# A decoder layer with soft-routed experts on one core: constants loaded from SyncE's queue, self scores in two parts and steps taken by sequence, ahead of the first expert

## The chip, the cores and the metric

The kernel runs on one core of one Trainium2 chip. The metric is device time in microseconds. Before the change the median of 7 runs is 2962.05 us (2960.71 to 2966.57). The engines are named as in the profile: PE (TensorE's matmuls), PEld (its weight loads), DVE (VectorE), ACT (ScalarE), POOL (GpSimd) and SP (SyncE). SP and ACT each have a queue from which they start DMA transfers.

## The reference

One decoder layer in float32 on x of 32 sequences x 100 tokens x 256, with a context of 361 tokens per sequence:

```python
x = x + self_attention(layernorm(x))          # 16 heads of 16, rope on q and k, causal
x = x + cross_attention(layernorm(x), ctx)    # 16 heads of 16, with biases, 361 keys
x = x + soft_moe(layernorm(x))                # 8 experts x 128 slots, hidden size 1024

def soft_moe(x):
    xn, sn = rmsnorm(x) * gamma, rmsnorm(slot_embeds) * slot_gamma
    logits = einsum("bnd,esd->bnes", xn, sn)
    dispatch = softmax(logits, axis=tokens)
    combine = softmax(logits, axis=(experts, slots))
    slots = einsum("bnd,bnes->besd", xn, dispatch)
    eo = gelu(slots @ w1 + b1) @ w2 + b2      # one w1 and w2 for each expert
    return einsum("bmd,bnm->bnd", eo, combine)
```

## The kernel before, in words

The 32 sequences form 8 groups of 4. For each group the kernel runs the 8 experts one after the other (`run_expert`, L1456): the first layer `ph` in 8 chunks of 512 columns, gelu on ACT into `hT`, the second layer `pe`, and `py`, which combines the result into x. A group needs its preparation first: self attention and cross attention of its 4 sequences, the logits `lt` (`prepare`, L1281) and the routing (`route`, L1376). The preparation of group g+1 is laid between the matmuls of group g's experts. Group 0 has no expert to lie behind: all of its preparation stands ahead of the first `ph`. This stretch is what the change is about. While it is recorded, `state["group"]` is -1.

**How the order is made.** The kernel is written as generators ("streams"): `self_attention`, `cross_softmax`, `crossing`, `cross_queries`, `cross_context`, and `prepare`. Each yields a `Need` (L299): the buffers that its next step reads and the PSUM banks that it takes. While the program is recorded, a planner keeps an estimated time for PE (`pe["t"]`) and a list of jobs for DVE, ACT, POOL and SP, each with an estimated duration, and writes the instructions out in the order of these estimates. `drive` (L344) takes the first stream in its list whose needs are met by the planner's time. `idle_from` (L82) says from when on the planner takes each engine to be free, and the numbers given to `load_raw` and `written` say when it takes a load to have landed. None of this costs time on the chip: it decides the order on each engine, and each engine then works through its order strictly, waiting on semaphores.

**The head.** `load_x(0)` is put on SP's list. `load_constants` (L459) starts 17 transfers from ACT's queue: four self attention weights (`rawWk`, `rawWq`, `rawWv`, `rawWo`), the rope table, five parts of `rows` (biases and gammas), four cross attention weights (`xwWk` and so on), two bias rows for all partitions, and the slot embeddings `se`. SP starts x of group 0 and 1 and the contexts. The DMA starts use eight completion semaphores in turn: the built program lets the start of a transfer wait until the transfer with the same semaphore, the eighth before it over both queues, has landed. PE transposes the raw weights (`turn_raw`, L445), the first context (`ps_cT`) and the first normalized sequence (`ps_xhT`), and ACT copies the last two out of PSUM.

**Self attention of a sequence** (`self_attention`, L862): `turned` (layer statistics on DVE and POOL, `xh` on POOL, `ps_xhT` on PE, its copy on ACT), `rotation` (`ps_qk`, then rope on DVE and POOL and `rotk` on ACT), `self_v` (`ps_v`), `self_scores` (L747), `self_turn` (`ps_pT`), `self_values` (`ps_av`) and `project_out` (`ps_o`). `self_scores` takes both PSUM pairs (`sc0`, `sc1`, two banks each, 8 heads each) and issues its 8 matmuls (fp32, so two passes each) over the four 32-row strips of PE, q = 0 to 3 for each of two chunks; then for each half: mask (`p`) and maximum on DVE, subtraction on POOL, exp on ACT, sum on DVE.

**Cross attention of a sequence**: `cross_context` makes keys and values (`ps_cT`, `ps_kT`, `ps_xv`), `cross_queries` the queries (`ps_xq`, `xqT`), and `cross_softmax` the scores in four "quads"; for a quad each of two halves takes a PSUM pair, has a maximum on DVE (`xnmax`) and two exps on ACT. For the first four sequences PE transposes the result (`ps_xpT`, 12 transposes a quad, copied by DVE, ACT, DVE); for all later ones DVE transposes it in PSUM into `xt` (one buffer), and two DMAs through DRAM (`xd`, `xpT`) lay it out. `crossing` multiplies by the values (`ps_xav`), projects (`ps_o`) and starts the tokens' statistics, which end with `xn` on POOL.

**The tail.** After the fourth crossing: `xn`, `ps_xhT`, `xnT`, `ps_lt` with maxima `mx`, transposes of the logits into both PSUM pairs, `cnm`, `diag`, `ps_nm`, then `route` for expert 0: exps, the sum `sm` and its reciprocal on DVE, `dT` on POOL, `pd`, `disp`, `sl`, `slT`, and then `ph`. L1588 drives this routing alone.

`near` (L857) limits how far ahead of the current group a stream may go: with the group at -1, one sequence into group 1, whatever the caller asks for.

## Time and profile before

| | |
|---|---|
| median of 7 runs | 2962.05 us |
| the profiled execution | 2963.34 us |
| its span, first to last instruction | 2961.6 us |
| granted TensorE clock, mean | 0.995 |
| PE busy, share of the span | 2911.1 us, 98% |
| PEld busy | 2035.9 us, 69% |
| DVE busy | 1367.9 us, 46% |
| ACT busy | 1234.9 us, 42% |
| POOL busy | 555.9 us, 19% |
| `ph` and `pe` matmuls, busy | 964.2 us and 1000.8 us |
| first `ph` starts | 220.83 us |

A line of a view by time gives start and duration in us, engine, source line, operation, the tiles written and read, their shapes, the count of instructions merged, and in brackets the idle time of that engine before them and what ended it. "ACTq" and "SPq" are the engines' sequencers starting a DMA. In a view by stages each engine has its busy time and its count of instructions; a granted clock of 0.5 means that TensorE ran at half its full rate. Busy times of PE are those of pipelined matmuls whose ends are modelled. Helpers record most instructions, so that nearly all matmuls carry line L268 and all transposes L272; the tile names tell them apart.

### The profile page before, as it was taken

Reading aid. Unit: us, or ns where it says so; the run is one execution under the profiler, and the core shown is the slowest. Engines: PE = TensorE matmul, PEld = TensorE weight load, DVE = VectorE, ACT = ScalarE, POOL = GpSimd, SP = SyncE. Lnnn points to the kernel's source line nnn. Section 1 sums busy time; section 2 is a strip of 40 time slices with the busy share of each in tenths; the row PEclk is TensorE's granted clock in tenths of the full one; section 3 lists DMA queues with packets and bytes.
Section 4 is the critical chain, followed back from the end, with each engine's and each line's share of the span. In section 5 each row is a group of like instructions: output and inputs, shape, how many; then the busy total and the mean of one; then the engine's idle time right before and its main releaser. Section 6 shows DMA issues by size and latency. Waiting matters only on the chain.

```text
span 2961.6 us, 42941 instructions
## 1 busy us (share of the span) xinstructions
PE 2911.1 (98%) x17393; PEld 2035.9 (69%) x17393; DVE 1367.9 (46%) x2719; ACT 1234.9 (42%) x2662; POOL 555.9 (19%) x722
## 2 busy tenths in 40 slices
PE   6989999999999999999999999999999999999999
PEld 5756766767667676677667666677676766677676
DVE  5764554546443554436444355444554345422121
ACT  3554444444443444434444444433444434433331
POOL 3413231032101221013210222002321021000000
PEclk9989999999999999999999999999999999999999
DMA  3012433334351343414343243433344234422221
GB/s 111 12 70 69 166 103 121 133 117 169 109 179 68 130 148 125 157 58 151 133 156 119 98 150 126 147 111 119 123 156 141 92 105 162 167 72 71 72 75 52
DMA packets 191574, 343.58 MB, mean 116 GB/s; under 512 B 8104, under 2 KB 160656, under 8 KB 191376
## 3 DMA queue, kind: packets, MB, share of 16 engines
q1 hardware_dynamic: 187632, 337.18, 33.3%
q10 hardware_dynamic: 3744, 3.65, 0.4%
q8 instruction: 138, 2.26, 0.3%
q14 instruction: 60, 0.49, 0.0%
HBM read 249.44 MB, written 91.36 MB: 115 GB/s over the span
## 4 chain that ended last, share of the span: by engine, by line
PE 95%; ACT 2%; DVE 1%; DMA 1%; POOL 1%; issue 0%; SPq 0%; ACTq 0%; DVEq 0%; POOLq 0%
PE pe L268 31%; PE ph L268 30%; PE sc L268 4%; PE sl L268 4%; PE py L268 4%; PE ps_lt L268 3%; PE ps_xv L268 3%; PE ps_kT L268 3%; PE ps_xav L268 2%; PE ps_qk L268 2%; PE ps_o L268 2%; PE ps_pT L272 1%; PE pd L272 1%; PE sc L272 1%; PE ps_xq L268 1%; PE ps_v L268 1%
## 5 line engine op out<-in xcount | busy, mean ns | idle before, releaser
L268 PE MATMUL pe<-w,hT 128*128 128x256 f32 x4096 | 1000.8, 383 | 0.0
L268 PE MATMUL ph<-slT,w 128*128 128x512 f32 x2048 | 964.2, 599 | 1.6 <-ACT hT L1479 1.4
L268 PEld LDWEIGHTS pe<-w,hT 128*128 128x128 f32 x4096 | 742.1, 190 | 156.4 <-issue 52.7
L1479 ACT ACTIVATE hT<-ph,cols 128x512 f32<-128x512 f32 x512 | 350.7, 687 | 799.1 <-PE ph L268 798.9
L268 PEld LDWEIGHTS ph<-slT,w 128*128 128x128 f32 x2048 | 372.0, 190 | 325.2 <-issue 291.2
L1049 ACT ACTIVATE sc<-sc,xnmax 128x361 f32<-128x361 f32 x448 | 237.8, 531 | 146.0 <-DVE xnmax L1039 138.8
L1039 DVE TENSOR_REDUCE xnmax<-sc 128x2 f32<-128x722 f32 x256 | 222.2, 904 | 162.7 <-PE sc L268 162.1
L1063 DVE STREAM_TRANSPOSE xt<-sc 128x384 f32<-128x384 f32 x448 | 231.8, 556 | 23.6 <-ACT sc L1049 18.2
L608 POOL TENSOR_SCALAR ve<-bnmv 100x1 f32<-100x1 f32 x96 | 27.8, 290 | 904.8 <-DVE bnmv L605 904.6
L1417 POOL TENSOR_TENSOR dT<-dT,ri 128x400 f32<-128x400 f32 x64 | 54.6, 853 | 721.4 <-DVE ri L1414 720.3
L1531 DVE SCALAR_TENSOR_TENSOR x<-py,cinv,x 100x256 f32<-100x256 f32 x256 | 112.7, 477 | 153.0 <-PE py L268 152.1
L1409 DVE TENSOR_REDUCE sm<-dT 128x4 f32<-128x400 f32 x64 | 34.7, 543 | 264.5 <-ACT dT L1400 264.5
L787 POOL TENSOR_TENSOR p<-p,nmax 100x800 f32<-100x800 f32 x64 | 96.5, 1524 | 315.4 <-DVE nmax L780 312.4
L1508 DVE TENSOR_TENSOR eo<-pe,b 128x512 f32<-128x512 f32 x128 | 87.6, 685 | 129.1 <-PE pe L268 128.8
L268 PEld LDWEIGHTS sl<-disp,xn 100*128 100x128 f32 x1024 | 135.7, 194 | 8.1 <-issue 1.3
L268 PE MATMUL sl<-disp,xn 100*128 100x128 f32 x1024 | 136.7, 277 | 0.9 <-DVE disp L1430 0.9
L1446 DVE TENSOR_SCALAR slT<-sl,cols 128x512 f32<-128x512 f32 x128 | 95.4, 745 | 84.3 <-PE sl L268 83.5
L268 PE MATMUL py<-eo,cT 128*100 128x256 f32 x512 | 131.5, 379 | 0.8 <-DVE eo L1508 0.8
L268 PE MATMUL sc<-kT,xqT 32*128 32x361 f32 x1024 | 124.6, 514 | 3.3 <-DVE xt L1063 2.0
L770 DVE TENSOR_TENSOR p<-sc,causal 100x800 f32<-100x800 f32 x64 | 60.4, 985 | 137.8 <-PE sc L268 137.8
L428 ACT ACT_TABLE_LOAD x93 | 119.3, 1283 | 1.6
L268 PEld LDWEIGHTS py<-eo,cT 128*100 128x100 f32 x512 | 85.4, 167 | 50.0 <-issue 29.0
(144 smaller groups left out, 3237.8 us busy)
## 6 DMA issues: line engine op xcount, KB each, us to landing
w<-in_L_ffn_w_dram SPq DMA_DIRECT2D x128, 1024.0 KB
xd<-xt SPq DMA_DIRECT2D x112, 768.0 KB
xpT<-xd SPq DMA_DIRECT2D x112, 768.0 KB
ctx<-in_ctx_dram SPq DMA_DIRECT2D x32, 256.0 KB
b<-in_L_ffn_b_dram SPq DMA_DIRECT2D x64, 128.0 KB
ctx<-in_ctx_dram SPq DMA_DIRECT2D x32, 105.0 KB
x<-in_x_dram SPq DMA_DIRECT2D x8, 400.0 KB
out_dram<-x SPq DMA_DIRECT2D x16, 200.0 KB
```

The lines of the kernel that those rows point to most:

```text
L268: nc.tensor.matmul(out, lhsT=lhsT, rhs=rhs, **kw)
L272: nc.tensor.transpose(out, in_, identity)
L428: act(0.2, lambda: nc.scalar.activation(spare, mhalf[:1, :1], f), [], [], table=table, prio=2)
L770: lambda i=i, hs=hs: nc.vector.tensor_tensor(p.get()[:, hs, :].rearrange("n (q h) k -> n q h k", q=2), sc[i].get()[:S, :, : HG * S].rearra ...
L787: lambda hs=hs: nc.gpsimd.tensor_tensor(p.get()[:, hs, :], p.get()[:, hs, :], nmax.get()[:, hs].unsqueeze(2).to_broadcast([S, HPC, S]), AL ...
L1039: lambda nm=nm, sc=sc: nc.vector.tensor_reduce(nm.get(), sc.get()[:, :, :SK], axis=AX.X, op=ALU.max, negate=True),
L1049: nc.scalar.activation(to[:, :SK], sc.get()[:, i, :SK], AF.Exp, bias=nm.get()[:, i : i + 1], accum_out=sums.get()[:, c, q, r : r + 1],)
L1063: nc.vector.transpose(t_.get()[:, :, :, 2 * t + i, :].rearrange("p j c u -> p c j u"), sc.get()[:, i, : NKB * P].rearrange("p (c u j) -> p ...
L1446: lambda dc=dc, sl=sl: nc.vector.tensor_scalar(slT.get()[:, dc, : nb * NS], sl.get()[:, : nb * NS], cols.ap[:, NGM + dc : NGM + dc + 1], N ...
L1479: lambda h=h, ph_=ph_, hc=hc: nc.scalar.activation(h.get()[:, :n], ph_.get()[:, :n], AF.Gelu, bias=cols.ap[:, e * NHC + hc : e * NHC + hc ...
L1508: lambda eo=eo, po=po, m=m: nc.vector.tensor_tensor(eo.get()[:, :m], po.get().rearrange("p (i d) -> p i d", i=2)[:, :m], b2.unsqueeze(1).t ...
L1531: lambda b=b, i=i: nc.vector.scalar_tensor_tensor(xs[g].get()[:, b, :], py[:S, i, :], k.ci.get()[:, b : b + 1], xs[g].get()[:, b, :], ALU. ...
```

## The change

- `load_constants`: ACT's queue starts `rawWk`, `rawWq` and the rope table only. The other 14 transfers go to SP's queue, in another order: `rawWv`, `xwWk`, the five parts of `rows`, `rawWo`, `xwWv`, the two bias rows, `xwWq`, `xwWo`. The slot embeddings become a job of SP (`load_slots`), and stand in the built program behind x of group 1 and the second context. x of group 0 and the first context are started ahead of the constants.
- `self_scores` becomes a generator. For group -1 it takes one PSUM pair at a time and issues the four matmuls of each half by themselves; for later groups both halves are issued as before.
- `drive` takes, among the streams that could go on, the one whose next step belongs to the lowest sequence (steps that belong to none count as 0), not the first in the list. It serves the stretch ahead of the first expert and the ends of later experts; the filling between an expert's matmuls keeps the list's order.
- `near` allows the caller's distance in group -1 too: self attention may begin up to three sequences into group 1.
- The routing ahead of the first expert is driven together with the other streams.
- `idle_from` and the landing times that the planner assumes are changed.

In the built program 1003 matrix instructions stand ahead of the first `ph`, where 987 did: those of the sixth sequence's `ps_xhT`, `ps_qk`, `ps_v` and half of its scores are added. The total is unchanged. Three quads of the fifth sequence stand between `ps_lt` and `pd`, where they stood ahead of `ps_lt`.

```diff
@@ -79,7 +79,7 @@
     COL, PIPE, HOP, LOAD = 0.00084, 0.25, 0.15, 1.28
     pe = {"t": 0.0, "slow": 1.25}
     waiting = {e: [] for e in ("DVE", "ACT", "POOL", "SP")}
-    idle_from = {"DVE": 0.0, "ACT": 8.0, "POOL": 6.0, "SP": 0.0}
+    idle_from = {"DVE": 0.0, "ACT": 3.0, "POOL": 5.0, "SP": 0.0}
     tables = {"now": None, "gelus": 0}
 
     class Buf:
@@ -283,6 +283,7 @@
             p, tag = self.pools[(len(self.past) - 1) % len(self.pools)]
             return p.tile([P, 512], F32, tag=tag, name=name)
 
+    at = {}
     rings = {
         "small": Banks([(ps_m, "mm"), (ps_b, "big")]), "big": None,
         "pairs": Kept(
@@ -302,7 +303,7 @@
 
         def __init__(self, *reads, banks=1, pairs=0, exps=None, when=None, t=0.0):
             self.reads, self.banks, self.pairs = reads, banks, pairs
-            self.exps, self.when, self.t = exps, when, t
+            self.exps, self.when, self.t, self.seq = exps, when, t, 0
 
         def time(self):
             items = [w for b in self.reads for w in b.writes]
@@ -319,8 +320,8 @@
     class Steps:
 
 
-        def __init__(self, it):
-            self.it, self.need, self.result = it, Need(banks=0), None
+        def __init__(self, it, seq=None):
+            self.it, self.need, self.result, self.seq = it, Need(banks=0), None, seq
 
         def blocked(self):
             return self.it is None or (self.need.when is not None and not self.need.when())
@@ -336,6 +337,7 @@
             reads = self.need.reads
             try:
                 self.need = next(self.it)
+                self.need.seq = at.get(self.seq, 0)
             except StopIteration as end:
                 self.it, self.result = None, end.value
             for b in reads:
@@ -348,7 +350,7 @@
             run()
             ready = [s for s in streams if s.fits()]
             if ready:
-                ready[0].step()
+                min(ready, key=lambda s: s.need.seq).step()
             else:
                 advance(*(s.time() for s in streams))
         return goal.result
@@ -435,12 +437,17 @@
         return t.rearrange("k (m r d) -> k m r d", r=2, d=DK)
 
 
-    def load_raw(nm, at):
+    def load_raw(queue, nm, at):
         raw = R["hT"].new(f"raw{nm}")
         v = raw.get().rearrange("p (c d) -> p c d", c=ND)
-        nc.scalar.dma_start(out=v, in_=a[f"L0_attn_{nm}"].rearrange("(c p) d -> p c d", p=P))
+        queue.dma_start(out=v, in_=a[f"L0_attn_{nm}"].rearrange("(c p) d -> p c d", p=P))
         raw.written(at)
         raws[nm] = raw
+
+    def load_cross(nm, at):
+        w = wT["x" + nm] = fixed([P, ND, D], f"xw{nm}")
+        nc.sync.dma_start(out=w.ap, in_=a[f"L0_xattn_{nm}"].rearrange("(c p) o -> p c o", p=P))
+        w.written(at)
 
     def turn_raw(nm):
 
@@ -458,11 +465,11 @@
 
     def load_constants():
 
-        load_raw("Wk", 5.5)
-        load_raw("Wq", 8.0)
+        load_raw(nc.scalar, "Wk", 5.0)
+        load_raw(nc.scalar, "Wq", 6.5)
         nc.scalar.dma_start(out=rope, in_=a["rope"].rearrange("p (m f) n -> p m f n", f=2))
-        load_raw("Wv", 11.0)
-        load_raw("Wo", 12.5)
+        load_raw(nc.sync, "Wv", 9.0)
+        load_cross("Wk", 10.0)
         rows = Buf(ap=one.tile([P, P], F32, name="rows"))
         for r0, src in (
             (BQ, a["L0_xattn_bq"].rearrange("(c p) -> c p", p=P)),
@@ -471,20 +478,25 @@
             (NGM, a["L0_ffn_norm_gamma"].rearrange("(c p) -> c p", p=P)),
             (SGM, a["L0_ffn_slot_norm_gamma"].rearrange("(c p) -> c p", p=P)),
         ):
-            nc.scalar.dma_start(out=rows.ap[r0 : r0 + src.shape[0], :], in_=src)
-        rows.written(14.0)
-        for k, nm in enumerate(("Wk", "Wq", "Wv", "Wo")):
-            w = wT["x" + nm] = fixed([P, ND, D], f"xw{nm}")
-            nc.scalar.dma_start(
-                out=w.ap, in_=a[f"L0_xattn_{nm}"].rearrange("(c p) o -> p c o", p=P)
-            )
-            w.written(15.5 + 1.5 * k)
-        nc.scalar.dma_start(out=bvB, in_=a["L0_xattn_bv"].partition_broadcast(P))
-        nc.scalar.dma_start(out=boB, in_=a["L0_xattn_bo"].partition_broadcast(P))
+            nc.sync.dma_start(out=rows.ap[r0 : r0 + src.shape[0], :], in_=src)
+        rows.written(13.0)
+        load_raw(nc.sync, "Wo", 14.0)
+        load_cross("Wv", 15.0)
+        nc.sync.dma_start(out=bvB, in_=a["L0_xattn_bv"].partition_broadcast(P))
+        nc.sync.dma_start(out=boB, in_=a["L0_xattn_bo"].partition_broadcast(P))
+        load_cross("Wq", 17.5)
+        load_cross("Wo", 18.5)
         se = Buf(ap=wpool.tile([P, NE, D], F32, tag="w1", name="se"))
-        nc.scalar.dma_start(out=se.ap, in_=a["L0_ffn_slot_embeds"].rearrange("e s d -> s e d"))
-        se.written(26.0)
         return rows, se
+
+    def load_slots(se):
+        job(
+            "SP", 0.4,
+            lambda: nc.sync.dma_start(
+                out=se.ap, in_=a["L0_ffn_slot_embeds"].rearrange("e s d -> s e d")
+            ),
+            [], [se], lag=8.0,
+        ).deps.append(18.0)
 
     def make_constants():
 
@@ -750,18 +762,28 @@
         p = R["p"].new()
         sums, nmax, rinv = R["sums"].new(), R["nmax"].new(), R["rinv"].new()
         qT = t.get().rearrange("p (m c n) -> p m c n", m=2, c=ND)[:, 0]
-        sc = [rings["pairs"].new("sc") for _ in range(2)]
-        for c in range(ND):
-            for q in range(NQ):
-                rows_ = slice(q * 32, (q + 1) * 32)
-                matmul(
-                    sc[q // 2].get()[:S, q % 2, c * 2 * S : (c + 1) * 2 * S],
-                    lhsT=qT[rows_, c, :],
-                    rhs=kT.get()[rows_, c, :, :],
-                    share=NQ, start=True, stop=True,
-                )
-        parts = []
+        sc, parts = {}, []
+        pairs_ = ((0,), (1,)) if state["group"] < 0 else ((0, 1),)
+
+        def issue(ts):
+            for i in ts:
+                sc[i] = rings["pairs"].new("sc")
+            for c in range(ND):
+                for i in ts:
+                    for q in (2 * i, 2 * i + 1):
+                        rows_ = slice(q * 32, (q + 1) * 32)
+                        matmul(
+                            sc[i].get()[:S, q % 2, c * 2 * S : (c + 1) * 2 * S],
+                            lhsT=qT[rows_, c, :],
+                            rhs=kT.get()[rows_, c, :, :],
+                            share=2 * len(ts), start=True, stop=True,
+                        )
+
         for i in range(2):
+            for ts in pairs_:
+                if ts[0] == i:
+                    yield Need(t, kT, banks=0, pairs=len(ts), exps=(4.0, 8.0))
+                    issue(ts)
             hs = slice(i * HPC, (i + 1) * HPC)
             part, s1, m1 = p.part(), sums.part(), nmax.part()
             parts.append(part)
@@ -857,7 +879,7 @@
     def near(b, ahead):
 
         last = FIRST[state["group"] + 1] + SIZES[state["group"] + 1]
-        return b < last + (ahead if state["group"] >= 0 else 1)
+        return b < last + ahead
 
     def self_attention(rows):
 
@@ -883,11 +905,11 @@
 
         yield from begin(0)
         for b in range(B):
+            at["self_attention"] = b
             xhT, t, kT = begun.pop(b)
             yield Need(xhT, wT["Wv"])
             self_v(xhT)
-            yield Need(t, kT, banks=0, pairs=2, exps=(4.0, 8.0))
-            p, parts, wide = self_scores(t, kT)
+            p, parts, wide = yield from self_scores(t, kT)
             if b == 0:
                 yield Need(raws["Wo"])
                 turn_raw("Wo")
@@ -1139,6 +1161,7 @@
     def cross_queries():
 
         for b in range(B):
+            at["cross_queries"] = b
             yield free(lambda: near(b, 1) and b in selfed and b < 2 + len(queried))
 
             def bias(b=b):
@@ -1155,6 +1178,7 @@
     def cross_context():
 
         for b in range(B):
+            at["cross_context"] = b
             yield free(lambda: near(b, 1))
             cT, keys[b] = yield from context(b)
             yield free(lambda: state["valued"] >= b - 1)
@@ -1164,6 +1188,7 @@
     def cross_softmax():
 
         for b in range(B):
+            at["cross_softmax"] = b
             for i, (c, r) in enumerate(QUADS):
                 n = b * len(QUADS) + i
                 yield free(
@@ -1270,6 +1295,7 @@
     def crossing():
 
         for b in range(B):
+            at["crossing"] = b
             g, i = WHERE[b]
             yield free(lambda: g <= state["group"] + 1)
             if i == 0:
@@ -1560,13 +1586,17 @@
 
     state = {"group": -1, "valued": -1, "crossed": -1, "turned": 0, "flipped": 0, "routed": NE, "columns": False, "spad": spad}
     load_x(0, 4.5)
+    load_ctx(0, 6.5)
+    pe["t"] = 1.5
+    run()
     rows, se = load_constants()
     make_constants()
-    load_ctx(0, 9.0)
+    load_slots(se)
+    idle_from["SP"] = 12.0
     load_x(1, 14.0)
     state["slots"] = Steps(slots(se))
     streams = [
-        Steps(it)
+        Steps(it, it.__name__)
         for it in (
             self_attention(rows), cross_softmax(), crossing(), cross_queries(), cross_context()
         )
@@ -1585,7 +1615,7 @@
     rings["small"], rings["big"] = Banks([(ps_m, "mm")], past[0::2]), Banks([(ps_b, "big")], past[1::2])
     pe["slow"] = 1.0
     routing = Steps(route(groups[0], 0))
-    ready = drive(routing, routing)
+    ready = drive(routing, routing, *order())
     w = first["w"]
     todo = [(g, e) for g in range(NG) for e in range(NE)]
     for i, (g, e) in enumerate(todo):
```

## The prediction

> **What bounds the kernel now.** I read the busy time by stage first, then the head and the tail of the first stage in order of time. By stage (length; busy us and instructions of PE, PEld, DVE, ACT, POOL; granted clock; DMA share; GB/s):
>
> ```profile
> 0.00:18.60 18.60, 4.00 (x16) 2.96 (x16) 5.21 (x8) 2.33 (x4) 6.47 (x20) 1.00 0.76 223
> ...
> 27.70:40.00 12.30, 7.86 (x49) 5.42 (x49) 8.65 (x16) 6.17 (x22) 6.73 (x6) 0.96 0.00 1
> 40.00:60.00 20.00, 16.91 (x135) 14.88 (x135) 13.50 (x28) 5.91 (x14) 9.24 (x11) 0.77 0.39 132
> 60.00:100.00 40.00, 38.09 (x412) 27.35 (x410) 34.84 (x69) 25.36 (x78) 15.95 (x18) 1.00 0.01 2
> ...
> 180.00:197.00 17.00, 12.45 (x107) 7.39 (x105) 12.53 (x25) 10.16 (x32) 3.43 (x7) 0.97 0.37 138
> 197.00:220.80 23.80, 17.34 (x73) 15.24 (x74) 10.14 (x20) 7.45 (x14) 1.88 (x2) 0.64 0.34 116
> 220.80:400.00 179.20, 179.20 (x1146) 123.40 (x1145) 95.32 (x191) 80.95 (x179) 54.44 (x66) 0.99 0.33 112
> ```
>
> From 220.8 us, where the first expert's first layer starts, PE is busy without a gap: of 2740.8 us only about 9 are idle, 5.3 of them after the last expert's second layer has begun. The time is therefore the start of the first expert plus the PE work left. Only two things move it: an earlier start, or work taken out of the part behind it. Ahead of 220.8 us PE is idle for 41.4 us, 14.6 of them before 18.6 us and 11 after 180 us, and its granted clock falls to 0.77 and 0.64. The head, in order of time:
>
> ```profile
> 2.31 0.71 ACTq L441 DMA_DIRECT2D rawWv<-in_L_attn_Wv_dram  x1
> ...
> 11.33 0.59 PE L272 MATMUL ps_xhT<-ident,xh 100*128 100x100 f32 x2 [0.90 <-POOL xh L639]
> 12.48 0.24 ACTq L474 DMA_DIRECT2D rows<-ffn_slot_norm_gamma_dram  x1
> ...
> 16.23 1.28 ACT L938 ACT_TABLE_LOAD   x1 [16.23 <-DMA xwWq<-in_L_xattn_Wq_dram]
> 18.23 0.34 ACT L627 COPY xhT<-ps_xhT 128x200 f32<-128x200 f32 x1
> 18.63 2.03 PE L268 MATMUL ps_qk<-xhT,wTWq 128*128 128x100 f32 x8 [6.70 <-ACT xhT L627]
> ```
>
> The reader is to see that PE had transposed the first sequence by 11.92 us, and that its copy out of PSUM began only at 18.23, because ACT was still starting loads until 16.2. The tail, in order of time:
>
> ```profile
> 188.87 1.11 PE L268 MATMUL ps_o<-xwWo,xoT 128*100 128x256 f32 x4
> 194.26 1.24 POOL L1262 TENSOR_SCALAR xn<-x,bnmv,r 100x256 f32<-100x256 f32 x1
> 197.18 8.51 PE L268 MATMUL ps_lt<-xnT,snT 128*128 128x200 f32 x32 [1.24 <-ACT xnT L627]
> 198.99 1.98 DVE L1063 STREAM_TRANSPOSE xt<-sc 128x384 f32<-128x384 f32 x4 [3.74 <-DMA xd<-xt]
> 215.85 0.69 DVE L1430 COPY disp<-pd 100x512 f32<-100x512 f32 x1 [2.18 <-PE pd L272]
> ```
>
> From the end of the last crossing's projection (189.95) to the first expert (220.83) runs one chain of 30.9 us through all engines, with little beside it.
>
> **Head.** ACT now starts three loads, the third ending at 2.3 us, and loads its table behind them. What is late next is xhT: its transposes end at 11.92 as before (POOL's statistics, its 1.38 us clearing of vpad and xh are unmoved; Wk, Wq, rope, x and ctx stay ahead of the rest). With 0.34 for the copy, ps_qk starts at 12.3 instead of 18.63: **-6.3**. Bounds: -5, should Wq come 1.3 us behind what the 3.2 us between its transposes (8.11) and ps_xhT hide; -7, because x of group 1 (400 KB) leaves the first eight transfers.
>
> SP's queue takes over 14 starts, each 0.24 to 0.71 us, and the built program makes each wait for the landing of the transfer eight before it. Behind the waiting ones stand x of group 1 (not needed before 90 us), the second context (31.47 - 6.3 = 25.2 us), and the slot embeddings. Rows can start once rope has landed (its follower started at 9.03) and land 1.5 us later (12.48 to 14.00 for the follower of the last row), so by 10.6, against a need at 23.0 - 6.3 = 16.7. Tightest are the slot embeddings: 5.1 MB must have moved, which at the 282 to 375 GB/s of the busiest 1.5 us slices is 14 to 18 us; the present order, with slices at 109 and 166 GB/s between, ends at some 24 us. I estimate 20 to 23, against a need at 28.11 - 6.3 = 21.8. ACT's squares have 2.4 us to spare (its idle time ahead of the next ctxT copy), so I cost it at 0; 3 us later than that would cost 3.
>
> ACT's 14 removed starts last 6.4 us together, but they held ACT for 13.9 us, since each waited for a landing; the path gets 6.3. [...]
>
> **28 to 46 us.** Two-part scores let the first half's mask, maximum and subtraction on POOL start some 0.8 us earlier, and POOL now does xh of the second sequence before rn (1.65 us). But ps_qk stands behind four ps_sn transposes that need rn and four scalings: relative to the old times rn ends at 38.9, four scalings of 0.31 end at 40.2, ps_sn at 41.1, against 42.7: **-1.6**, bounds 0 and -3 (the clock was 0.50 here, after 4.2 us without work; the gap is now split in two).
>
> **Order by sequence.** In PE's order, what stands ahead of the last crossing's ps_o loses two cross scores (16 matmuls at 27.6/152 us: 2.9), a kT (2.4), an xq (0.9), two thirds of an xv (1.7) and half a cT (0.4), and gains a ps_qk (1.9 at full clock): 6.4 less, **-6**. Its price is cover: with fewer sequences under way PE has less to do while DVE and ACT work. I followed the first crossing by rows: from the projection of sequence 0's self attention to that of its crossing I get 31 us, against 42.8 now, of which 12.0 is PE work that moves behind it: no change. A quad keeps DVE 2.9 us (two xnmax at 0.9, two copies at 0.57), ACT 3.1 us (four exps, one copy), and PE 2.5 to 3 us plus the self work. I take **+1**, bounds -4 (all the idle time of 93 to 139 gone) and +12.
>
> **Two-part scores on PE.** Both halves of a cross score side by side last 0.89 (88.09 us), one half alone 0.88 (62.53), so a self score whose halves come apart costs another 0.87. Of the first six, two certainly come apart, one second half behind the first expert's start: **+1**, bounds 0 and +3.5.
>
> **Tail.** POOL now does the fifth sequence's ve, rstd, xh and bias (2.8 us) among xn's seven steps: +2.7. PE has work until xn, so ps_lt should run at full clock: 5.68 us (139.26) instead of 8.51, -2.8. DVE gets a mask, maximum and sum (2.95), six xnmax (5.5) and four more transposes (2.0) ahead of disp: 10.5 us, for which its idle time from 197.2 to 215.9 (10 us) has room for about two thirds: +3.7. Together **+3.6**, bounds -3 (all of it hidden) and +8. One transposition into the single xt buffer stands ahead of route's sum and waits for the transfer before it, as in the row with 3.74 above; its cover is the two cnm, diag and two xnmax (4.7 us) against 3.4 to 5.6 us of transfer. [...]
>
> **Work moved ahead.** The sixth sequence's xhT (0.3), ps_qk (1.9), ps_v (0.86) and half its scores (0.45) now stand before the first expert: the part behind it shrinks by **-3.5**, bounds -2.5 and -4.
>
> **The rest**: the same instructions in a PE-bound order, 0, bounds +-2. Sum: -6.3 - 1.6 - 6 + 1 + 1 + 3.6 - 3.5 = -11.8, so -12. On the profiled execution (2963.34, its span 2961.6 and 1.74 around it) that is 2951.3; the median shown is 1.3 lower, so I say 2950.
>
> **Rivals.**
> - *Head alone* (0.15): new idle time eats the reordering, 9 us over four sequences. For it: depth first, xhT, xq and xqT of a sequence run with little beside them. Against: the first crossing's sum. -3, so 2959; up to 2962.
> - *All of it* (0.15): the tail hides the scores and its clock stays up, the middle loses its idle time: -19, so 2943.
> - *Slower* (0.06): the quads become a chain. Alone a quad lasts 0.88 + 0.92 + 1.3 + 1.53 + 1.05 = 5.7 us, and two PSUM pairs must overlap it. If one exp pair of 1.3 us is exposed in each of 16 quads, +20.8 - 12 = +9, so 2971. It decides from 18/16 = 1.1 us of new PE idle time per quad. Against: DVE and ACT are busy under 90% and 65% of the time from 60 to 100 us.
> - *Forecast* (0.64): 2943 to 2956.
>
> Measurement tells 0.2% (5.9 us) from no change. Faster: 0.64 + 0.15 = 0.79; within: 0.15; slower: 0.06. The range 2941 to 2959 leaves out the slower case and the outer halves of its neighbours.
>
> **What would show it.** Head: ACT's table load at 2 to 4 us, ps_qk near 12.3. Middle: last crossing's ps_o near 175, and PE idle time from 60 to 175 near 10 us. Tail: ps_lt of 5.7 us, 34 us from that ps_o to the first expert, which starts near 212 us. Wrong if PE waits for xqT, exps or xh between 40 and 175 us for over 20 us, if ACT waits for the slot embeddings, or if PE idles behind the first expert.

## The result, and the profile after

The changed kernel takes **2971.68 us** (median of 12 runs, 2968.87 to 2973.99), where the one before took 2961.65 (median of 30 runs beside it, 2960.28 to 2966.57): a ratio of 1.0031, with a 95% interval of 1.0024 to 1.0039. It is slower by 10.0 us, where 11.8 less were forecast. The profiled execution has a span of 2972.2 us.

The stages after, with the columns of the table of stages before (length; busy us and instructions of PE, PEld, DVE, ACT, POOL; granted clock; DMA share; GB/s):

```profile
20.00:40.00 20.00, 15.70 (x87) 12.06 (x85) 11.96 (x25) 9.50 (x30) 7.59 (x7) 0.83 0.23 73
40.00:60.00 20.00, 14.66 (x110) 9.75 (x111) 15.90 (x29) 8.80 (x26) 8.88 (x11) 0.74 0.40 132
60.00:100.00 40.00, 33.23 (x320) 25.34 (x318) 24.19 (x50) 19.20 (x59) 13.06 (x18) 0.88 0.04 10
...
190.00:232.20 42.20, 34.27 (x180) 24.26 (x170) 24.68 (x47) 18.09 (x44) 9.38 (x14) 0.74 0.22 79
232.20:400.00 167.80, 167.80 (x1060) 113.54 (x1059) 86.09 (x173) 73.76 (x161) 46.50 (x58) 0.99 0.36 121
```

From 60 to 100 us PE was busy 38.1 us with 412 instructions at a clock of 1.00; now it is busy 33.2 us, with 320 instructions, at 0.88. Behind the first `ph`, now at 232.25, everything is as before (2739.9 us against 2740.8). The whole loss lies ahead of it. The head did what was said, as the order of time shows:

```profile
2.32 1.28 ACT L960 ACT_TABLE_LOAD   x1 [2.32 <-issue]
...
11.88 0.59 PE L272 MATMUL ps_xhT<-ident,xh 100*128 100x100 f32 x2 [1.11 <-POOL xh L651]
...
12.51 0.33 ACT L639 COPY xhT<-ps_xhT 128x200 f32<-128x200 f32 x1 [1.24 <-PE ps_xhT L272]
```

The copy follows its transposes at once, and `ps_qk` starts at 12.89, 5.7 us earlier. The tail, PE's rows in order of time, from the last crossing's projection to the first expert:

```profile
191.45 1.03 PE L268 MATMUL ps_o<-xwWo,xoT 128*100 128x256 f32 x4
...
201.58 5.68 PE L268 MATMUL ps_lt<-xnT,snT 128*128 128x200 f32 x32
207.19 0.89 PE L268 MATMUL sc<-kT,xqT 32*128 32x361 f32 x8
211.85 3.63 PE L272 MATMUL sc<-ident,lt 128*100 128x128 f32 x16 [3.77 <-ACT sc L1071]
...
226.19 1.09 PE L272 MATMUL pd<-ident,dT 128*100 128x128 f32 x4
228.07 3.79 PE L268 MATMUL sl<-disp,xn 100*128 100x128 f32 x16 [0.78 <-DVE disp L1456]
...
232.25 1.89 PE L268 MATMUL ph<-slT,w 128*128 128x512 f32 x2
```

`ps_lt` runs at full clock (5.68 us, granted 1.00), as forecast. But a quad of the fifth sequence now stands between it and the transposes of the logits. It holds both PSUM pairs, so the transposes wait 3.8 us for its exps, and then run at half clock (16 in 3.63 us, granted 0.50). The tail lasts 40.8 us where it lasted 32.0.

**An account that adds up.** The span is PE's idle time plus its busy time. Before: 50.5 + 2911.1. After: 52.5 + 2919.7. The same instructions keep PE busy 8.6 us longer. Summed over stretches of 2 us up to 270 us, busy time times (1 - granted clock) is 12.4 us before and 24.1 after. The ends of PE's rows are modelled, and 3 us between these two differences are not placed. The same figures for other runs (first `ph`; PE's idle and busy time over the whole span; busy time lost to the clock; all of the profiled execution, which lies up to 2.5 us from the median):

| kernel | median us | first ph | idle | busy | lost to clock |
|---|---|---|---|---|---|
| before | 2961.65 | 220.8 | 50.5 | 2911.1 | 12.4 |
| loads_only | 2956.17 | 213.6 | 43.7 | 2910.7 | 12.3 |
| no_parts | 2959.58 | 224.9 | 47.1 | 2910.1 | 13.3 |
| seq_only_loads | 2967.93 | 221.7 | 52.3 | 2911.3 | 13.8 |
| loads_parts | 2973.08 | 229.3 | 55.3 | 2914.7 | 17.6 |
| issue_loads | 2979.09 | 236.7 | 59.1 | 2918.9 | 23.8 |
| no_near | 2969.59 | 226.4 | 53.1 | 2915.3 | 20.2 |
| after | 2971.68 | 232.2 | 52.5 | 2919.7 | 24.1 |
| warm_all | 2966.73 | 225.6 | 44.6 | 2920.2 | 13.6 |
| warm_before | 2957.91 | 212.6 | 42.5 | 2911.4 | 1.7 |
| warm_loads | 2949.72 | 206.6 | 36.5 | 2911.5 | 1.7 |

### The profile page after: what moved, and what is told of

The parts are those of the page before. It is cut to its first block, busy times and chain, and to the rows that moved or that the text cites. A ratio compares the mean times of both kernels' runs of the same rounds, so it can differ in the third digit from the quotient of the medians.

```text
span 2972.2 us, 42933 instructions
## 1 busy us (share of the span) xinstructions
PE 2919.7 (98%) x17393; PEld 2043.3 (69%) x17393; DVE 1368.6 (46%) x2719; ACT 1235.1 (42%) x2662; POOL 554.4 (19%) x722
## 4 chain that ended last, share of the span: by engine, by line
PE 94%; ACT 2%; DVE 2%; POOL 1%; DMA 0%; issue 0%; SPq 0%; DVEq 0%; ACTq 0%; POOLq 0%
PE pe L268 31%; PE ph L268 30%; PE sc L268 5%; PE sl L268 4%; PE py L268 4%; PE ps_lt L268 3%; PE ps_xav L268 3%; PE ps_kT L268 2%; PE ps_xv L268 2%; PE ps_qk L268 2%; PE ps_o L268 2%; PE ps_pT L272 1%; PE pd L272 1%; PE ps_av L268 1%; PE sc L272 1%; PE ps_xq L268 1%
## 5 line engine op out<-in xcount | busy, mean ns | idle before, releaser
L1085 DVE STREAM_TRANSPOSE xt<-sc 128x384 f32<-128x384 f32 x448 | 231.9, 556 | 18.3 <-ACT sc L1071 16.7
```

The lines of the kernel that those rows point to most:

```text
L1085: nc.vector.transpose(t_.get()[:, :, :, 2 * t + i, :].rearrange("p j c u -> p c j u"), sc.get()[:, i, : NKB * P].rearrange("p (c u j) -> p ...
```

## The experiments

Ratios are against the kernel before, run beside each, with 95% intervals.

### One part undone at a time

Theory A blamed the choice by sequence, theory B the routing driven with the other streams. `loads_only` undoes all four edits below; each of the others undoes one.

```diff
-                min(ready, key=lambda s: s.need.seq).step()      # no_seq
+                ready[0].step()
-    ready = drive(routing, routing, *order())                    # no_drive
+    ready = drive(routing, routing)
-        pairs_ = ((0,), (1,)) if state["group"] < 0 else ((0, 1),)   # no_parts
+        pairs_ = ((0, 1),)
-        return b < last + ahead                                  # no_near
+        return b < last + (ahead if state["group"] >= 0 else 1)
```

> The changed kernel with the first free stream taken again, self scores issued in one part, the look-ahead of group -1 back at one sequence and the first routing driven alone: of the change only the other load queue, the loads' order and the assumed times are left. Theory A (the choice by sequence leaves PE without cover in the middle) and theory B (the routing that shares PE with the fifth sequence lengthens the tail) both say that this keeps the 5.7 us that the first ps_qk starts earlier: 2956, with the first ph near 215. Rival (the head's gain is lost to later waits whatever the order is): 2961 or more, first ph near 220.

Measured: 2956.17, ratio 0.998 (0.9971 to 0.9989), first `ph` at 213.6. The loads keep the head's gain to the end.

> The changed kernel with the first free stream taken, not that of the lowest sequence. 1099 matrix instructions stand ahead of the first ph, 96 more than in the changed kernel, so that the first ph may come later at the same time of the whole. Theory A: the 8 to 9 us lost between the first and the third crossing come back, 2963; PE idle time from 40 to 180 us falls by 5 us or more and the granted clock from 60 to 140 us is back at 1.00. Theory B: no more than 2 us come back, 2970.

Measured: 2988.20, ratio 1.0086 (1.0072 to 1.0099). Taking the choice by sequence away costs 16.5 us more, so theory A falls as it stands: beside two-part scores, the choice by sequence helps. The tail alone is 31.7 us here, where it is 40.8 in the changed kernel.

> The changed kernel with the routing of the first expert driven alone, as before the change. Theory B: the tail from the last crossing's ps_o to the first ph falls from 40.8 to 32 to 34 us, the time to 2963 to 2965. Theory A: the tail is shorter but the work only moves behind the first ph, so 2969 to 2971; the middle is as slow as in the changed kernel.

Measured: 2981.09, ratio 1.0062 (1.0048 to 1.0076). Theory B falls too: the tail is 38.7 us, and the same wait of 3.8 us stands in it. The rest of the loss lies behind the first `ph`: PE idles 16.7 us there, where 9.8 are idle in the changed kernel, and one of the waits is for a quad's exps ahead of the next group's transposed logits (3.5 us near 590 us).

> The changed kernel with both halves of a self score issued together, taking both PSUM pairs at once. Rival C (the two-part scores cost PE 0.87 us each and hold the pairs): 2966 to 2968. Theories A and B: within 2 us of the changed kernel, 2970 to 2973, with the same idle time in the middle.

Measured: 2959.58, ratio 0.9993 (0.9984 to 1.0002). The rival that had been given 4 to 6 us gets 12.1. The two-part scores are the largest single cost.

> The changed kernel with the look-ahead of group -1 back at one sequence: 987 matrix instructions ahead of the first ph, not 1003. If the work moved ahead is worth the 3.5 us forecast: 2975. If it costs as much ahead of the first ph as it saves behind it: 2970 to 2973. If it stands in the way of the tail: under 2969.

Measured: 2969.59, ratio 1.0026 (1.0018 to 1.0035). The work moved ahead is not worth 3.5 us; without it the median is 2.1 us lower, with intervals that overlap.

### One part alone, beside the loads

> The loads and the choice by sequence, and nothing else of the change: self scores in one part, the look-ahead of group -1 at one sequence, the first routing alone. The chip has shown 2956.2 for the loads alone, and 2959.6 for all of the change but the two-part scores. Theory S (the choice by sequence binds self attention to the pace of the crossings and costs cover by itself): 2958 to 2962, crossings from 60 to 190 us later than in the run with the loads alone. Theory P (it is the two-part scores that cost, and the choice by sequence brings the crossings forward as forecast): 2950 to 2954.

Measured: 2967.93, ratio 1.0019 (1.0010 to 1.0028): 11.8 us over the loads alone, with 8.6 us more PE idle time. The last crossing's `ps_o` comes at 184.6, against 182.75 with the loads alone, and its tail lasts 37.1 us against 30.8. The longer tail goes with this edit: in the kernels without added transposes it lasts 37.1 to 42.6 us in all nine that choose by sequence, and 30.3 to 34.9 in the seven that don't.

> The loads and the two-part self scores, and nothing else of the change (first free stream, look-ahead of one sequence, first routing alone). Theory P (a self score that needs one PSUM pair at a time takes pairs from the cross scores, and its second half holds up the start of the next sequence): 2964 to 2972, first ph 8 us or more later than the 213.6 of the loads alone. Theory I (the parts cost only together with the choice by sequence, whose streams are short of cover): 2956 to 2958.

Measured: 2973.08, ratio 1.0036 (1.0023 to 1.0048): 16.9 us over the loads alone, first `ph` at 229.3. Each of the two edits costs by itself. They don't add up: all of the change is 15.5 us over the loads. PE's rows show what the parts do. With the loads alone, between the second and the third self score:

```profile
45.17 0.94 PE L268 MATMUL sc<-rotk,ropet 32*100 32x200 f32 x16
47.87 0.39 PE L272 MATMUL ps_xhT<-ident,xh 100*128 100x100 f32 x2 [1.76 <-POOL xh L651]
...
55.49 0.88 PE L268 MATMUL sc<-kT,xqT 32*128 32x361 f32 x4 [0.24 <-DVE xqT L1022]
...
58.05 0.88 PE L268 MATMUL sc<-kT,xqT 32*128 32x361 f32 x4
...
60.76 1.29 PE L268 MATMUL sc<-kT,xqT 32*128 32x361 f32 x8
...
67.48 1.59 PE L268 MATMUL sc<-rotk,ropet 32*100 32x200 f32 x16
```

And with the two-part scores beside the loads:

```profile
44.31 0.95 PE L268 MATMUL sc<-rotk,ropet 32*100 32x200 f32 x16
53.96 0.59 PE L272 MATMUL ps_xhT<-ident,xh 100*128 100x100 f32 x2 [8.69 <-POOL xh L651]
...
65.57 0.95 PE L268 MATMUL sc<-rotk,ropet 32*100 32x200 f32 x16
67.58 1.77 PE L268 MATMUL sc<-kT,xqT 32*128 32x361 f32 x8 [1.07 <-DVE p L792]
```

Two things are to be seen. The cross scores (`sc<-kT,xqT`) that stood between the self scores are gone: with two more behind 60.76, six halves of quads ran there, now none does, and the first crossing's `ps_o` moves from 86.2 to 106.8. And PE waits 8.7 us for `xh`: masks and maxima of both halves (3.8 us on DVE) and the subtraction on POOL (3.0 us) stand ahead of the layer statistics. Also, both halves in a row still last 0.95 us for 16 matmuls, where one half alone lasts 0.92 (8 matmuls, at 200.73 us in the changed kernel), so they run side by side as before.

Inside the change the same edit shows otherwise. `no_parts`, where both halves ask for their pairs at once, has the third self score ahead of the first crossing's projection:

```profile
67.36 0.94 PE L268 MATMUL sc<-rotk,ropet 32*100 32x200 f32 x16
...
83.88 1.11 PE L268 MATMUL ps_o<-xwWo,xoT 128*100 128x256 f32 x4
```

The changed kernel has it behind:

```profile
79.84 1.03 PE L268 MATMUL ps_o<-xwWo,xoT 128*100 128x256 f32 x4
...
84.25 0.95 PE L268 MATMUL sc<-rotk,ropet 32*100 32x200 f32 x16
```

There the first crossing comes 4.0 us earlier with the parts, and the second 16.1 later (119.70 against 103.58). So what is read from the rows above holds beside the loads; why the parts cost 12.1 us inside the change is not shown by it.

### Which of the two it is: order on DVE and POOL, or the PSUM pairs

```diff
+            early = state["group"] < 0 and b > 0 and near(b + 1, 3)     # parts_begin
-            p, parts, wide = yield from self_scores(t, kT)
+            p, parts, wide = yield from self_scores(t, kT, begin(b + 1) if early else iter(()))
         for i in range(2):
+            if i == 1:
+                yield from ahead
```

> The changed kernel, in which, from the second sequence on, the next sequence's statistics, transposes and ps_qk are begun between the two halves of a self score instead of behind the second half. Theory P in its narrow form (the 6 us that the second ps_xhT between 49 and 55 us is late come from there): the first crossing's ps_o near 74, first ph 4 to 8 us earlier than 232.3, the time 2962 to 2968. If the start of the next sequence is not what is late: 2970 to 2974.

Measured: 2980.81, ratio 1.0059 (1.0046 to 1.0072). The first crossing came at 77.1 (79.8 in the changed kernel), but the fourth at 196.1 (191.45). The narrow theory falls, and the edit costs 9.1 us more.

In `stats_all`, `stats_loads_parts` and `stats_loads`, `bn_stats` and `bn_aggr` get the priority 0.5 instead of 1 in group -1, so that they go ahead of the maxima:

> The loads and the two-part self scores (2973.1), with one thing more: ahead of the first expert the layer statistics on DVE (0.6 us) go ahead of the maxima of a self score, where they stood behind masks and maxima of both halves (3.8 us), with 3.0 us of subtractions ahead of xh on POOL in consequence. Theory O (the parts cost by this order on DVE and POOL): PE's wait of 8.7 us for xh after the second self score falls to 3 to 6, the first crossing comes 4 us or more earlier than 106.8, the time is 2963 to 2968. Theory R (they cost by taking PSUM pairs from the cross scores): 2971 to 2974.

Measured: 2978.73, ratio 1.0055 (1.0041 to 1.0069). PE still waits 8.4 us for `xh`, so the edit didn't reach the wait it was made for, and the time lies above both ranges.

> The changed kernel (2971.7) with the layer statistics ahead of the maxima before the first expert. Theory O: the wait of 7.5 us in all for xh between 40 and 190 us halves and the clock from 46 to 110 us stays over 0.9; 2964 to 2968. Theory R: 2970 to 2973.

Measured: 2971.89, ratio 1.0034 (1.0021 to 1.0046). All four crossings come 2.7 to 3.1 us earlier in the profile, whose span is 2.7 shorter; the median is the same. Theory O gets no more than that.

> Control: the loads alone (2956.2) with the layer statistics ahead of the maxima before the first expert. There they stand ahead of masks and maxima already at the second score, so theory O expects no difference: 2954 to 2958. If the order of the statistics is an improvement of its own, whatever the parts do: under 2953.

Measured: 2961.02, ratio 0.9996 (0.9987 to 1.0005). The control is 4.9 us slower than the loads alone, which neither theory had. A change of order as small as this moves the time by that much.

`issue_loads` takes the pairs one at a time, and lists all other work after both halves:

```diff
+        for ts in pairs_:
+            yield Need(t, kT, banks=0, pairs=len(ts), exps=(4.0, 8.0))
+            issue(ts)
         for i in range(2):
-            for ts in pairs_:
-                if ts[0] == i:
-                    yield Need(t, kT, banks=0, pairs=len(ts), exps=(4.0, 8.0))
-                    issue(ts)
```

> The loads and the two-part scores (2973.1), but the work of DVE, POOL and ACT for both halves is listed only once both halves have been issued: the halves take PSUM pairs one at a time, and the layer statistics stand ahead of the masks again, as with scores in one part (2956.2). Theory O (the parts cost by the order on DVE and POOL): 2956 to 2960, PE's wait of 8.7 us for xh gone. Theory R (they cost because a score that needs one pair at a time goes ahead of the cross scores, whose sequence is then finished later): 2966 to 2974, the wait gone but the first crossing still after 100 us.

Measured: 2979.09, ratio 1.0050 (1.0037 to 1.0062). The wait for `xh` is back at 1.6 us, as theory O wants it, and the time is 22.9 us over the loads alone all the same, above the range of either theory. Three halves of quads run between the second and the third self score, and the first crossing comes at 111. Taking the pairs one at a time is enough to cost this beside the loads; theory R stands there in kind, not in size.

### The choice by sequence

```diff
-            at["self_attention"] = b                    # seq_lead
+            at["self_attention"] = b - 1
-                min(ready, key=lambda s: s.need.seq).step()       # cap_seq_loads
+                min(ready, key=lambda s: min(s.need.seq, 3)).step()
```

> The changed kernel, in which self attention counts as belonging to the sequence before its own, so that the choice by sequence lets it run one sequence ahead of the crossing. 1076 matrix instructions stand ahead of the first ph, 73 more, some 20 us of PE work. Theory S: PE idle time from 40 to 190 us, 26 us in the changed kernel, falls under 18 and the time to 2960 to 2965. If the binding is not the cause: 2970 or more.

Measured: 2974.23, ratio 1.0041 (1.0028 to 1.0053). From 40 to 190 us PE idles 23.5 us, where 21.5 are idle in the changed kernel (the 26 of the expectation were too many), and the first crossing comes at 94.3, not 79.8. Theory S in this form falls.

> The loads and the choice by sequence (2967.9), with the sequences from the fourth on counted alike, so that the fifth sequence's quads may go ahead of the fourth crossing's end as in the run with the loads alone. Theory Q (the choice by sequence costs in the tail, where a quad of the fifth sequence stands between ps_lt and the transposes of the logits and these wait for its exps): the tail from the last crossing's ps_o to the first ph falls from 37.1 to 31 to 33 us, the time to 2957 to 2962. If the loss comes from elsewhere: 2966 or more.

Measured: 2966.17, ratio 1.0016 (1.0007 to 1.0025), tail 39.0 us. The fifth sequence's quads now stand ahead of `ps_lt`, but PE waits there 5.6 us for a transposition into `xt`. Theory Q is not shown: what the choice by sequence loses in its tail wasn't given back by this edit.

### Is it the clock?

These kernels leave the order of every instruction as it is, and add transposes of the identity to the same bank just ahead of an instruction that PE waits with. The results are overwritten.

```diff
+    def keep(ps, n):
+        for _ in range(n):
+            nc.tensor.transpose(ps.get()[:, :P], ident, ident)
         ps = bank("ps_xhT")
+        keep(ps, n)
```

> The changed kernel with the same order of all its instructions and 80 transposes of the identity more, which PE may run while it waits and whose results are overwritten: 12 and 8 ahead of ps_xhT and ps_sn near 31 and 33 us, 10, 10 and 18 ahead of the ps_xhT near 48, 55 and 94 us, 4 ahead of the last xn's transposes, 6, 8 and 4 ahead of ps_nm, pd and sl. At full clock they last 0.13 us each, 10 us together, all in PE time that is idle now. Theory C (the reduced clock after these waits is what the time is lost to): the clock from 46 to 110 us stays near 1.00, the crossings come 4 to 8 us earlier, the time is 2962 to 2967. Rival (the chains through DVE, ACT and POOL set the time, and PE's clock is only along for the ride): 2970 to 2974.

Measured: 2966.73, ratio 1.0013 (1.0004 to 1.0021), so 5.0 us less than the changed kernel. PE's rows of the changed kernel from the second self score on:

```profile
48.65 0.39 PE L272 MATMUL ps_xhT<-ident,xh 100*128 100x100 f32 x2 [1.76 <-POOL xh L651]
...
51.83 1.59 PE L268 MATMUL sc<-kT,xqT 32*128 32x361 f32 x8 [0.48 <-DVE xqT L1022]
55.12 0.59 PE L272 MATMUL ps_xhT<-ident,xh 100*128 100x100 f32 x2 [1.70 <-POOL xh L651]
55.70 2.66 PE L268 MATMUL sc<-kT,xqT 32*128 32x361 f32 x8
58.29 2.82 PE L272 MATMUL ps_xpT<-ident,p 128*128 128x128 f32 x12
```

The same with the waits filled (L636 are the added ones):

```profile
44.37 1.31 PE L636 MATMUL ps_xhT<-ident 128*128 128x128 f32 x10
46.20 0.39 PE L272 MATMUL ps_xhT<-ident,xh 100*128 100x100 f32 x2 [0.52 <-POOL xh L660]
...
49.98 2.40 PE L636 MATMUL ps_xhT<-ident 128*128 128x128 f32 x10
52.66 0.40 PE L272 MATMUL ps_xhT<-ident,xh 100*128 100x100 f32 x2 [0.28 <-POOL xh L660]
...
54.84 1.53 PE L272 MATMUL ps_xpT<-ident,p 128*128 128x128 f32 x12
```

The 12 `ps_xpT` take 1.53 us where they took 2.82. They start 3.5 us earlier, of which 2.5 are from ahead of the second self score (43.49, not 45.94). The first filling works, the second less so: its 10 transposes last 2.40 us, and the clock is 0.50 from 50 to 52 us, but back at 1.00 from 54, not from 64. The crossings come 4.2, 6.8, 6.8 and 6.9 us earlier. So some 5.0 us of the changed kernel's time is paid to the clock. That is not the change's own share, since the kernel before gains from filling too (below); there nearly nothing is lost any more (1.7 us), here 13.6, of which 7.2 lie in the tail behind the wait for the quad, where the banks that PE would write are the ones held.

> The loads alone (2956.2), order unchanged, with 83 transposes of the identity in PE's waits: 14 and 8 near 31 and 33 us, 10 near 46 us, 10 ahead of the last xn's transposes, 6 ahead of ps_lt, 12 ahead of ps_nm, 18 ahead of pd, 5 ahead of sl. Theory C: ps_lt takes 5.7 us where it took 8.0, pd, sl and the first ph run at full clock, which is 4 to 5 us of the tail, and 1 to 2 us come from the gaps at 31 and 46 us: 2949 to 2953, below both kernels. Rival: 2955 to 2958.

Measured: **2949.72**, ratio 0.9960 (0.9947 to 0.9974): faster than both kernels. Its tail, PE's rows:

```profile
188.59 5.82 PE L268 MATMUL ps_lt<-xnT,snT 128*128 128x200 f32 x32
...
199.61 2.13 PE L636 MATMUL pd<-ident 128*128 128x128 f32 x18
202.83 0.64 PE L272 MATMUL pd<-ident,dT 128*100 128x128 f32 x4 [1.09 <-POOL dT L1456]
...
204.26 2.05 PE L268 MATMUL sl<-disp,xn 100*128 100x128 f32 x16 [0.24 <-DVE disp L1470]
```

`ps_lt` took 7.98 us without them, `sl` 3.75.

> The kernel before the change, order unchanged, with 87 transposes of the identity in PE's waits: 26 near 36 us, 10 near 53, 10 ahead of the last xn's transposes, 6 ahead of ps_lt, 12 ahead of ps_nm, 18 ahead of pd, 5 ahead of sl. Theory C: of the 12.4 us that a reduced clock costs PE's busy time, at least half shows in the time, 2954 to 2957; a filled version of before is then faster than the change. Rival (the gain of the filled kernels came with the new head): 2960 to 2963.

Measured: 2957.91, ratio 0.9982 (0.9973 to 0.9991): 4.2 us less, a little short of the 5 to 8 that theory C gave it, and outside the rival's 2960. A gain from filling shows in all three orders of the stretch that were filled (5.0, 6.5 and 4.2 us). Filled, the loads are 8.3 us ahead of the kernel before, and the changed kernel 8.8 behind it.

> The loads alone with filled waits (2949.7), in which the 10 transposes that stood behind the wait near 46 us, and cost 1.25 us of PE there, are put into it (11, ahead of the third sequence's ps_xhT). Theory C: 1 to 1.5 us less, 2948 to 2949. If PE's time there is covered anyway: 2949.5 to 2950.5.

Measured: 2949.57, ratio 0.9956 (0.9943 to 0.9968). No difference to `warm_loads`: those 10 transposes had not cost anything that counts.

## Why the prediction was wrong, step by step

- **Head, -6.3**: right. 5.7 at `ps_qk`; the loads alone give 5.8 at the end, with the second sequence's `ps_qk` at 34.69 against 42.71. ACT does wait 2.5 us for the slot embeddings, and this stayed covered. From the first to the second `ps_qk` (**28 to 46 us, -1.6**) the changed kernel gains 2.2, but not by the two-part scores that the prediction named: the loads alone, with scores in one part, gain 2.1 there, and the change without the parts 2.6. The number came out by luck.
- **Order by sequence, -6 and +1**: this is the step that failed first. The count of PE work was right (27 fewer matrix instructions are seen ahead of the last crossing's `ps_o`), and it was the wrong thing to count: PE's busy time ahead of it falls by 1.2 us, not by 6.4, and it came at 191.45, not near 175. "No change" for the first crossing had been worked out from rows at full clock, as 31 us; it takes 35.8. It still comes 13.4 us earlier than before, and that lead is lost in the next three (3.6, 8.6 and 3.8 us longer than before). Lost cover was put at one microsecond: from 40 to 190 us PE idles 21.5 us (11.9 before), and the clock takes another 12.1 (4.7 before). Beside the loads alone, the edit costs 11.8.
- **Two-part scores, +1**: the term was priced on the wrong resource. On PE the parts cost almost nothing (0.95 us for both in a row; one score, near 157 us, comes apart). Their price is in the order that the planner makes: 16.9 us beside the loads, where a score that needs one pair goes ahead of the cross scores, and 12.1 in the change, where the rows show another order and the way to the price stays open. The prediction had no bound that held this.
- **Tail, +3.6, bounds -3 and +8**: +8.8. The projection to `xn`'s transposes +2.3 (POOL was given +2.7). `ps_lt` -2.8, as said. From the end of the logits' transposes to `pd` +4.2 (DVE was given +3.7). Not in the sum at all: 5.7 us from the end of `ps_lt` to the end of those transposes, for the quad that holds both pairs (3.8 of wait, and the transposes at half clock, granted 0.50). (From `xn`'s transposes to `ps_lt` -0.5, behind `pd` 0: 8.8 in all.) The prediction had counted that quad's DVE work, and not what it holds.
- **Work moved ahead, -3.5**: 0.9 behind the first `ph`. Without the look-ahead the median is 2.1 us lower.
- **The clock** ran through the prediction as a gain (-2.8 in the tail) and as a reason for -1.6. That the idle time it allowed (up to +12) would be paid a second time in clock was missing. With the waits filled, 5.0 us of the changed kernel, 6.5 of the loads alone and 4.2 of the kernel before come back.
- **The slower rival** named 2971, and that is the time measured, but its mechanism is half of it. It wanted 1.1 us of new PE idle time per quad; there is 0.6 (9.6 over 16), and the clock adds 0.5 (7.4 over 16). Nor do the exps set it. The longest waits of PE from 40 to 190 us in the changed kernel (us in total, times, longest) are:

```profile
PE ps_xhT L272 <- POOL xh L651: 7.5, 5, 2.9
PE ps_xpT L272 <- ACT xpT L1130: 3.2, 3, 1.1
PE ps_pT L272 <- ACT xpT L1130: 2.6, 3, 0.9
PE ps_pT L272 <- DVE xpT L1130: 2.2, 3, 0.7
```

Normalized sequences, and copies out of PSUM: work that had others beside it before. The prediction's own test ("PE waits for xqT, exps or xh for over 20 us") was not met, since these waits add up to 9.3 us there: the rest are small waits of other kinds, and what the clock then takes. PE's idle time from 60 to 175 us is 13.0 us, where near 10 was forecast and 8.2 stood before.

**Open.** The single edits don't add up, and a control moved the time by 4.9 us, so the share of each can't be told apart further than above. What the choice by sequence costs by itself (11.8 us beside the loads) is placed only in part: in the profiled executions 6.3 of the 9.2 us between them lie in the tail, but neither the lead nor the cap gave it back. Nor is it shown how the two-part scores cost 12.1 us inside the change.

## What to carry to other kernels

In a stretch where PE idles now and then, price an edit in PE idle time twice: once as such, and once as the clock that was seen to follow it (21.5 us and 12.1 us from 40 to 190 us in the changed kernel, 11.9 and 4.7 in the one before); work that PE may do in its waits without holding anything gives some of the second part back (4.2 to 6.5 us here, with no instruction moved). Where a planner makes the order, an edit that lets a step ask for fewer buffers at once changes whose turn it is (16.9 us beside the loads). Of a step that is moved into a chain, count what it holds until it is done, not only its work.

## What the runs showed of the hardware

In the following stretches the granted clock fell to 0.50 behind waits of which none was longer than 2.86 us. In the changed kernel it is 0.50 from 50 to 62 us behind waits of 1.76 and 0.41 us, with two of 0.48 and 1.70 in that stretch, from 94 to 100 us after most of one of 2.86, and from 108 to 110 behind two of 0.74 and 0.86. In the kernel before, it falls near 196 us, in the third of three waits of 1.65, 1.25 and 1.24 us, ahead of `ps_lt` (0.54 from 196 to 198 us, 0.50 from 198 to 202). From 94 to 100 us PE is busy 5.56 of 6 us, and the clock stays at 0.50 all the same. What length or spacing of waits brings it down is not shown. With 83 added transposes, 11 us of PE work at 0.13 each, the loads alone lose 1.7 us to the clock, where they lost 12.3.

Two groups of four fp32 matmuls (8 records each in the rows) on different 32-row strips, issued one group behind the other, last 0.95 us together, as long as when they alternate (0.94), where one group alone lasts 0.92.
